# An FFN's inner layer in three-chunk rounds: a two-bank and a one-bank PSUM tile in turn, and an activation table named at the start

## The chip, the cores and the metric

The kernel runs on one core of a Trainium2 chip. The metric is the device time of one execution in microseconds, the median of several runs. The engines are named as the profile names them: PE (TensorE matmuls), PEld (TensorE weight loads), DVE (VectorE), ACT (ScalarE), POOL (GpSimd), SP (SyncE, which here issues most DMAs).

## The reference, cut to what matters

The input `x` has 4 images of 384 channels and 32 x 32 positions, so 1024 tokens per image. Two layers follow one another. Layer 0 is a selective scan in four directions (16 states per channel) with a GELU, then a mixture of four experts of which each token takes two. Layer 1 is self-attention with 8 heads, then a small FFN whose two weight matrices are Kronecker products:

```python
w_fc = jnp.kron(c_fc_1, c_fc_2)        # (1536, 32) x (1, 12)  -> (1536, 384)
w_proj = jnp.kron(c_proj_1, c_proj_2)  # (32, 1536) x (12, 1)  -> (384, 1536)
h = x @ w_fc.T
h = jax.nn.gelu(h, approximate=False)
out = h @ w_proj.T
```

The residual and a normalisation stand around each part. The change is in this last FFN. Because of the Kronecker form the kernel first folds 384 channels into 32 numbers per token (`z`), and the inner layer multiplies only those 32 numbers by the 1536 columns of `c_fc_1`.

## The kernel before, in words

Tokens are in the free dimension of the inner layer, in halves of 512 (`HF`), and the 1536 hidden units are 12 chunks (`FC`) of 128 partitions. One batch of the whole program is one image.

**The order of the work.** `scan_layer` (L192) walks over 32 units (image, direction, half). When the scan of an image ends, the function `between` (L1292) starts `tail_batch` of the image before it: experts, combine, attention and the last layers, while the next image's scan goes on. So the tails of images 0 and 1 run beneath the scans, that of image 2 straddles the end of the last scan, and that of image 3 comes last. The order on each engine is not written by hand: the whole program is handed to a planner that lays out a timeline with priorities when the kernel is built (`schedule_with_timeline_sim=True`, L1285). Parts inside `high_priority(offset=FORWARD)` go ahead of the scan's work whenever they are ready; routing (L603), the combine (L488) and the last layers (L495) are such parts. On an engine the instructions then run in that fixed order.

**Rooms and banks.** The tail draws its buffers from a `Room` (L88). On-chip buffers have tags with a number of buffers each: for images 0 to 2 `NARROW` (L78), with two `k12` buffers; for image 3 `WIDE` (L79), with three. PSUM has three tags: `s`, of two banks each (`two`, L107), `o` and `p`, of one bank each (`bank`, L104). Images 0 to 2 have one buffer of each tag (L84). The attention and last layers of image 3 have two of each (L85), which is all eight banks.

**The last layers** (`last_layers`, L1049). The attention's result is projected (L1083, `o_ps`), added to the tokens `xt` (L1087, a `k12` buffer that stays to the end), and normalised. `z` is made by L1091 to L1112. Then, for each half `i` of the tokens and for each group of six chunks, `hidden` (L1117) makes `hs`, a `k12` buffer: for three pairs of chunks, a pair of matmuls of 32 rows (L1123) into one two-bank tile of tag `s`, and one ACT copy of 1024 columns (L1127) into `hs`; then one ACT GELU over all 3072 columns (L1128), with a table load before it and one after it (`exp_again`, L141). Chunk `f` uses the rows `f % 4` of the 32-row strips. The six chunks of `hs` are then contracted into `f_acc` (tag `o`, L1136). After both groups, DVE copies `f_acc` to `fy` (L1141), and for each of the three channel blocks a one-bank tile `fo_ps` (tag `p`, L1143) takes 8 matmuls (L1146 and L1150), ACT copies it out (L1155) and a DMA stores it (L1156). There are thus four calls of `hidden` in an image and sixteen in the kernel.

Other users of tag `p` in the same room are the routing of the next image (`tt_ps`, L622; `cnt_ps`, L705), which runs beside the last layers of images 0 and 1, and the attention before them.

The other place that the change touches is the start of `Body.__init__`: ACT there issues the load of the packed constants `cols` (L123); `scan_layer` makes ACT issue the load of `wx` (L203), and the first activation is the exponential that makes `nega` (L206).

Of the kernel before, what the change touches and what calls it, by code (L numbers as in the profile page):

```python
# [87 lines left out]
class Room:  # L88


    def __init__(self, tc, ctx, name, bufs):
        self.tc, self.name, self.bufs = tc, name, bufs
        self.sb = ctx.enter_context(tc.tile_pool(name=name, bufs=1, reuse_waits="tile"))
# [17 lines left out]
def halves(i):  # L111
    return slice(i * HF, (i + 1) * HF)


class Body:
    def __init__(self, ctx, tc, a):
        self.tc, self.nc, self.a = tc, tc.nc, a
        nc = self.nc
        const = ctx.enter_context(tc.tile_pool(name="const", bufs=1))
        self.const = const  # L120

        self.cols = const.tile([P, NCOL], F32, tag="cols", name="cols")
        nc.scalar.dma_start(out=self.cols, in_=a["cols"])  # L123

        self.ident = const.tile([P, P], F32, tag="ident", name="ident")
        make_identity(nc, self.ident)
        self.ones = const.tile([P, P], F32, tag="ones", name="ones")
        nc.gpsimd.memset(self.ones, 1.0)
        self.eps5 = const.tile([P, 1], F32, tag="eps5", name="eps5")
        nc.gpsimd.memset(self.eps5, 1e-5)  # L130
        self.eps6 = const.tile([P, 1], F32, tag="eps6", name="eps6")
        nc.gpsimd.memset(self.eps6, 1e-6)

        self.minus1 = const.tile([P, 1], F32, tag="minus1", name="minus1")
        nc.gpsimd.memset(self.minus1, -1.0)

        self.c2sum = const.tile([P, 1], F32, tag="c2sum", name="c2sum")
        lo, hi = COL["c2"]
        nc.vector.tensor_reduce(self.c2sum, self.cols[:, lo:hi], AX.X, ALU.add)
# [909 lines left out]
    def last_layers(self, b, att, room):  # L1049
# [4 lines left out]
        nc, a = self.nc, self.a  # L1054
# [23 lines left out]
        for m in range(0, MB, 2):  # L1078
            ps = room.two("o_ps")
# [26 lines left out]
        ps = room.two("z_ps")  # L1106
# [8 lines left out]
        ng = 6  # L1115

        def hidden(i, at):  # L1117
            hs = room.tile([P, ng, HF], "k12", "hs")
            for f in range(at, at + ng, 2):
                ps = room.two("h_ps")  # L1120
                for o in range(2):
                    rows = slice((f + o) % nq * KR, ((f + o) % nq + 1) * KR)
                    nc.tensor.matmul(  # L1123
                        ps[:, o, :], fc1[rows, (f + o) // nq, :], z[rows, halves(i)],
                        start=True, stop=True,
                    )
                nc.scalar.copy(hs[:, f - at : f - at + 2, :], ps)  # L1127
            self.exp_again(nc.scalar.activation(hs, hs, AF.Gelu).ins)  # L1128
            return hs

        for i in range(NH):
            out = room.bank("o", "f_acc")
            for at in range(0, FC, ng):
                hs = hidden(i, at)
                for f in range(at, at + ng):
                    nc.tensor.matmul(  # L1136
                        out[f % nq * KR : (f % nq + 1) * KR, :], pj1[:, f, :], hs[:, f - at, :],
                        start=(f < nq), stop=(f >= FC - nq),
                    )
            y = room.tile([P, HF], "k4", "fy")  # L1140
            nc.vector.tensor_copy(y, out)  # L1141
            for c in range(DC):
                ps = room.bank("p", "fo_ps")  # L1143
                for j in range(HF // P):
                    cols = slice(j * P, (j + 1) * P)
                    nc.tensor.matmul(  # L1146
                        ps[:, cols], pj2[:, c * P : (c + 1) * P], y[:, cols],
                        start=True, stop=False,
                    )
                    nc.tensor.matmul(  # L1150
                        ps[:, cols], xt[:, i * (HF // P) + j, c * P : (c + 1) * P], self.ident,
                        start=False, stop=True,
                    )
                o = room.tile([P, HF], "k4", "out")
                nc.scalar.copy(o, ps)  # L1155
                nc.sync.dma_start(out=a["out"][b][c * P : (c + 1) * P, halves(i)], in_=o)  # L1156
# [229 lines left out]
```

## Time and profile before

| | |
|---|---|
| runs | 4482.89, 4482.44, 4480.09 us; median 4482.44 us |
| profiled execution | 4517.48 us, of which the span from the first to the last instruction is 4513.6 us |
| PE | 3440.6 us busy (76%), 13852 matmul instructions |
| DVE | 3010.8 us busy (67%) |
| POOL | 3037.0 us busy (67%) |
| ACT | 2534.3 us busy (56%) |
| L1123, the inner layer's matmuls | 192 instructions, two for each chunk of 512 columns |
| L1127, its copies | 48 of 1024 columns, 1010 ns mean |
| L1128, its GELUs | 16 of 3072 columns, 2763 ns mean, each with a table load of 1283 ns |
| last layers' `z` ready (L1112) | image 0 at 1891, 1 at 2992, 2 at 4135, 3 at 4450 us |

The busy time of an engine is what it spent in instructions, without its waits. The profiled execution is slower than the median of the runs by 35 us; its parts add up to its own time.

### The profile page before, as it was taken

To read this page: it belongs to the slowest core of one execution; us is meant where nothing else is said; L and a number is where in the kernel's file an instruction comes from. 1 tells how busy PE (TensorE), PEld (TensorE's weight loads), DVE (VectorE), ACT (ScalarE), POOL (GpSimd) and SP (SyncE) were. 2 spreads that over 40 slices of the span, in tenths; PEclk is the share of its full clock that TensorE was granted. 3 is DMA by queue.
4 is the path that set the end of the run, shared out by engine and by line. 5 is a ranking of instruction groups with operands and counts; after the bars stand their busy time and mean duration, and the time that the engine had idled before them with its cause. 6 is when DMAs were issued, how large, how long until landed. Compare 5 with 4: busy or idle time off the path is not lost. (4 is left out here: it accounts for less than half of the span.)

```text
span 4513.6 us, 46925 instructions
## 1 busy us (share of the span) xinstructions
PE 3440.6 (76%) x13852; PEld 1652.0 (37%) x13852; DVE 3010.8 (67%) x4344; ACT 2534.3 (56%) x4406; POOL 3037.0 (67%) x1467
## 2 busy tenths in 40 slices
PE   6545554479894787669998588757998689999796
PEld 2111121145552222225555222214555445556333
DVE  4999997878878977977877777896778520002102
ACT  4555554456665676466666577556666444334554
POOL 4999998788987877778988778878889510000100
PEclk7666665589996898669998699858999789999897
DMA  4444554477886533457779443445787543344200
GB/s 119 118 123 118 146 136 106 137 230 209 231 240 181 149 84 104 130 159 226 210 220 275 137 114 101 115 139 170 232 244 232 169 157 115 107 127 153 75 16 15
DMA packets 404361, 684.81 MB, mean 152 GB/s; under 512 B 50944, under 2 KB 206464, under 8 KB 404096
## 3 DMA queue, kind: packets, MB, share of 16 engines
q1 hardware_dynamic: 395360, 656.16, 50.3%
q0 software_dynamic: 8192, 25.17, 1.7%
q8 instruction: 111, 1.82, 0.2%
q14 instruction: 154, 1.26, 0.1%
q10 hardware_dynamic: 544, 0.40, 0.0%
HBM read 561.47 MB, written 120.06 MB: 151 GB/s over the span
## 5 line engine op out<-in xcount | busy, mean ns | idle before, releaser
L420 POOL TENSOR_TENSOR bx<-dtr,bcs 128x1024 f32<-128x1024 f32 x768 | 1797.8, 2366 | 227.7 <-PE acc L455 103.5
L429 ACT ACTIVATE da<-dtr,nega 128x512 f32<-128x512 f32 x1536 | 1045.5, 691 | 1039.4 <-DVE bx L441 569.0
L448 POOL TENSOR_TENSOR bx<-bx,bcs 128x1024 f32<-128x1024 f32 x384 | 903.6, 2358 | 211.8 <-DVE bx L434 88.0
L455 PE MATMUL acc<-bx,sel 128*32 128x512 f32 x3072 | 511.8, 713 | 312.4 <-POOL bx L448 248.8
L879 PE MATMUL h_ps<-xc,w 128*128 128x256 f32 (+1 forms) x3168 | 680.1, 370 | 61.7 <-DVE xc L861 31.5
L895 PE MATMUL y_ps<-w,hs 128*128 128x384 f32 x1824 | 649.9, 509 | 49.8 <-ACT hs L888 44.1
L879 PEld LDWEIGHTS h_ps<-xc,w 128*128 128x128 f32 x3168 | 557.2, 200 | 253.4 <-issue 120.4
L434 DVE TENSOR_TENSOR_SCAN bx<-da,carry,bx 128x512 f32<-128x512 f32 x384 | 474.0, 1269 | 118.6 <-POOL bx L420 65.5
L434 DVE TENSOR_TENSOR_SCAN bx<-da,bx 128x512 f32<-128x512 f32 x384 | 452.2, 1209 | 129.2 <-POOL bx L420 70.3
L434 DVE TENSOR_TENSOR_SCAN da<-da,carry,bx 128x512 f32<-128x512 f32 x384 | 476.5, 1273 | 67.9 <-ACT da L429 62.6
L441 DVE TENSOR_TENSOR bx<-da,bcs 128x512 f32<-128x512 f32 x768 | 509.8, 679 | 3.8
L434 DVE TENSOR_TENSOR_SCAN da<-da,bx 128x512 f32<-128x512 f32 x384 | 456.3, 1218 | 60.7 <-ACT da L429 44.2
L895 PEld LDWEIGHTS y_ps<-w,hs 128*128 128x128 f32 x1824 | 352.3, 198 | 341.7 <-issue 86.4
L992 ACT ACTIVATE ex<-s_ps 128x512 f32<-128x512 f32 x512 | 299.4, 591 | 274.9 <-PE s_ps L987 259.9
L987 PE MATMUL s_ps<-w 64*128 64x512 f32 x1024 | 308.4, 674 | 83.1 <-ACT ex L992 74.2
L1077 POOL TENSOR_TENSOR xt<-xt,wb 128x3072 f32<-128x3072 f32 x4 | 26.8, 6708 | 477.5 <-DMA w<-in_w 345.5
L1036 PE MATMUL o_acc<-ex,vt 128*64 128x512 f32 x1024 | 295.6, 658 | 0.8 <-ACT att L1044 0.8
L455 PEld LDWEIGHTS acc<-bx,sel 128*32 128x32 f32 x3072 | 77.7, 117 | 596.0 <-POOL bx L448 363.8
L884 ACT ACTIVATE hs<-h_ps,bb 128x256 f32<-128x256 f32 (+1 forms) x528 | 194.0, 447 | 128.8 <-PE h_ps L879 128.5
L899 DVE TENSOR_TENSOR y<-y_ps,bb 128x384 f32<-128x384 f32 x76 | 41.6, 548 | 237.6 <-PE y_ps L895 237.6
L913 POOL DMA_INDIRECT got<-made,g_pos x64 | 60.8, 950 | 192.4 <-PE f_acc L1136 159.1
L987 PEld LDWEIGHTS s_ps<-w 64*128 64x128 f32 x1024 | 81.1, 192 | 266.8 <-ACT ex L992 149.1
(216 smaller groups left out, 4021.9 us busy)
## 6 DMA issues: line engine op xcount, KB each, us to landing
w<-in_w SPq DMA_DIRECT2D x352, 576.0 KB
dtr<-dd SPq DMA_DIRECT2D x1536, 128.0 KB
bcs<-rows SPq DMA_DIRECT2D x512, 128.0 KB
dd<-one_e SPq DMA_DIRECT2D x96, 256.0 KB
dd<-mag SPq DMA_DIRECT2D x96, 256.0 KB
rows<-zero SPq DMA_DIRECT2D x76, 192.0 KB
xs<-rows SPq DMA_DIRECT2D x32, 384.0 KB
made<-y SPq DMA_DIRECT2D x32, 384.0 KB
```

Source lines behind the costliest of these rows:

```text
L420: pool = nc.gpsimd.tensor_mul(bx, dtr[q][1], bc[:, 0].unsqueeze(1).to_broadcast([P, 2, HF])).ins
L429: nc.scalar.activation(da, dtr[q][0][:, j, :], AF.Exp, scale=nega[:, col : col + 1])
L434: nc.vector.tensor_tensor_scan(run(h), run(da), run(bx[:, j, :]), 0.0 if first else hold, ALU.mult, ALU.add,)
L441: dve = nc.vector.tensor_mul(bx[:, j, :], h, cg).ins
L448: pool = nc.gpsimd.tensor_mul(bx, bx, cg.unsqueeze(1).to_broadcast([P, 2, HF])).ins
L455: nc.tensor.matmul(acc[lo : lo + DB, :], sel, out[q][:, j, :], start=(g == 0), stop=(g == NG - 1),)
L879: nc.tensor.matmul(ps[:, r, :], w1[(f + r) // wf][:, c, (f + r) % wf * P : ((f + r) % wf + 1) * P], xc[:, c, :], start=(c == 0), stop=(c = ...
L884: nc.scalar.activation(hs[:, f + r, :], ps[:, r, :], AF.Identity, bias=bb[:, f + r : f + r + 1])
L895: nc.tensor.matmul(out[:, :D], hs[:, f, t * P : (t + 1) * P], w2[f // wf][:, f % wf, :], start=(f == 0), stop=(f == FC - 1),)
L987: nc.tensor.matmul(ps[:, o, :], w[rows, j * P : (j + 1) * P], w[rows, halves(i)], start=True, stop=True,)
L992: ins = nc.scalar.activation(ex[:, o, :], ps[:, o, :], AF.Exp, scale=HD**-0.5, accum_out=sums[:, t, 2 * j + o, i : i + 1],).ins
L1036: ins = nc.tensor.matmul(out[cols, :], made[t][1][:, j, cols], ex[:, o, :], start=(j == 0), stop=(j == MB - 1),).ins
```

## The change

There are two edits. The first puts a load of the table set `natural_log_exp_and_others` at the head of ACT's program. The second takes the six chunks of `hidden` in the pattern two, one, two, one. The twos use a two-bank tile of tag `s`, the ones a one-bank tile of tag `p`; each tile is copied by one ACT instruction, so that a call of `hidden` has two copies of 1024 columns and two of 512 in place of three of 1024. The matmuls, the GELU and everything behind it are the same.

```diff
@@ -119,6 +119,8 @@
         const = ctx.enter_context(tc.tile_pool(name="const", bufs=1))
         self.const = const
 
+
+        nc.scalar.preload_act_table_set("natural_log_exp_and_others")
         self.cols = const.tile([P, NCOL], F32, tag="cols", name="cols")
         nc.scalar.dma_start(out=self.cols, in_=a["cols"])
 
@@ -1116,15 +1118,22 @@
 
         def hidden(i, at):
             hs = room.tile([P, ng, HF], "k12", "hs")
-            for f in range(at, at + ng, 2):
-                ps = room.two("h_ps")
-                for o in range(2):
+
+            f = at
+            while f < at + ng:
+                if (f - at) % 3 == 0:
+                    ps = room.two("h_ps")
+                else:
+                    ps = room.bank("p", "h_ps").unsqueeze(1)
+                n = ps.shape[1]
+                for o in range(n):
                     rows = slice((f + o) % nq * KR, ((f + o) % nq + 1) * KR)
                     nc.tensor.matmul(
                         ps[:, o, :], fc1[rows, (f + o) // nq, :], z[rows, halves(i)],
                         start=True, stop=True,
                     )
-                nc.scalar.copy(hs[:, f - at : f - at + 2, :], ps)
+                nc.scalar.copy(hs[:, f - at : f - at + n, :], ps)
+                f += n
             self.exp_again(nc.scalar.activation(hs, hs, AF.Gelu).ins)
             return hs
 
```

## The prediction

> **What bounds the kernel now.** First the page: the busy tenths in 40 slices of the span.
>
> ```profile
> PE   6545554479894787669998588757998689999796
> ...
> DVE  4999997878878977977877777896778520002102
> ...
> POOL 4999998788987877778988778878889510000100
> ```
>
> Two regimes. Up to about 3600 us POOL and DVE carry the scan, and the tails of images 0 and 1 run beneath it. After that POOL and DVE are nearly empty and PE is full, until the last layers of image 3. Does the FFN beneath the scan count at all? For this I read the chain that ended last around the FFN of image 1 (start, us, what).
>
> ```profile
> 3058.33 1.01 ACT hs L1127
> ...
> 3060.66 2.76 ACT hs L1128
> ...
> 3100.63 0.15 SPq L833
> ...
> 3101.10 4.65 DMA xs<-rows
> ```
>
> It does, at least in part: the chain runs through the FFN's copies and GELUs (and, in between, through the scan's DVE work) into the weight load and the gather with which the next image's experts begin. An FFN that ends sooner lets them begin sooner. Then the view of the inner layer's matmuls, what they wait for (us, times).
>
> ```profile
> L1123 PE MATMUL h_ps<-z,wc x192: 587/848/1218, 1892.6 to 4487.5; 32*128 32x512 f32 x192
> ...
>   ACT hs L1127: 100.9, 36
> ```
>
> The matmul stands behind the copy of the tile before it: PE and PEld together sat 100.9 us before L1123 for L1127. Last the timeline of the final stage.
>
> ```profile
> 4463.01 1.93 ACT L1127 COPY hs<-h_ps 128x1024 f32<-128x1024 f32 x2
> ...
> 4465.31 1.37 PE L1123 MATMUL h_ps<-z,wc 32*128 32x512 f32 x8
> 4466.72 1.01 ACT L1127 COPY hs<-h_ps 128x1024 f32<-128x1024 f32 x1 [1.78 <-PE h_ps L1123]
> 4467.75 1.28 ACT L1128 ACT_TABLE_LOAD   x1
> ...
> 4469.04 2.76 ACT L1128 ACTIVATE hs<-hs 128x3072 f32<-128x3072 f32 x1
> ```
>
> ACT makes two copies, then idles 1.78 us: the third pair found no free bank and was queued behind 3.63 us of L1136 on PE. Also: eight instructions (four chunks, four row strips) take 1.37 us, where the row of four (one pair) takes 1.13. Chunks of different strips run side by side.
>
> **The change part by part.** All against the profiled 4517.48 us.
>
> *The table load at the start.* The load is there already: 1.28 us at 1.69, before the first exponential (L206). It moves ahead of the two DMA issues of ACT's queue (0.75 and 1.20), which go 1.28 later. `cols` then lands near 5.1 instead of 3.8; c2sum, dsum and nega follow it. Cover: the first matmul waits for `u` until 8.05, and `wx` is not read before 34.6. If that cover went, it would cost 1.3. I take 0, bounds 0 and +1.3.
> The Trainium skill ("ScalarE: Activation LUTs", What ACT_TABLE_LOAD costs) counts 2.66 us for a switch, with a drain; here the GELU starts 1.29 us after its load starts (4467.75, 4469.04). By the page `cols` would land near 6.5, still before 8.05, so the sum is 0 by either.
>
> *The copies.* Two copies of 1024 in a row take 1.93, so 0.965 each; two of 512 in a row (L1155 at 4484.20) take 1.08, so 0.54. A call: 3 x 0.965 = 2.90 before, 2 x 0.965 + 2 x 0.54 = 3.01 after. The 0.11 is inside the sums below.
>
> *Last layers of image 3* (two `s`, two `p`). All six chunks find a bank, so PE can fill them during the GELU before. ACT is then the only chain: load 1.28, copies 3.01, load 1.28, GELU 2.76 = 8.33 from GELU to GELU. They now start at 4458.94, 4469.04, 4479.22, 4491.31: gaps of 10.10, 10.18, 12.09. That saves 1.8 and 1.9, and up to 3.8 in the last, where the outputs of the first half (L1155) are copied too and share tag `p`; I take 2.0 there. In the first call four chunks end together (4451.30 to 4453.39), the other two by 4455.46, copies to 4456.97, load: GELU at 4458.3, 0.7 sooner. Sum **-6.4**. Best case -8.2. Worst case, banks of tag `p` given strictly in program order: the third call's second single chunk waits for three `fo_ps`. After the GELU: L1136 3.65, `fy` to 4.39, two `fo_ps` of 1.92 each from 4.95, copy 0.6, the third 1.92 and 0.6, then chunk 1.13, copy 0.54, load 1.28, about 14.3 where it is 7.4 now: +6.9, so 0.6 in all (-0.7 - 1.8 + 6.9 - 3.8).
>
> *Image 2* (one `s`, one `p`, one `hs`: `xt` holds the other `k12` buffer). The last call runs its three copies from 4212.36 to 4220.42, 8.06 us, PE cold (pair 2.08). With a pair and a single ready: copy 1.0, pair 2.08 beside the single's copy, copies 1.0 and 0.58, about 4.7, plus two 0.58 copies of the combine between them: 5.9, so -2.2. The third call's last chunk waits for `fo_ps`, whose third ends on PE at 4199.8: copy 0.58, chunk 1.13, copy 0.58, load 1.28, GELU 4203.4 instead of 4201.74, +1.7. The first two calls stand among the experts' matmuls on a full PE: three bursts of 1.13 become two of about 1.25 (between 1.13 and 1.37), -0.9 each. Sum **-2.3**; bounds -6 (no such wait, and both late calls save 2.2) and +11 (below).
>
> *Images 0 and 1, beneath the scan.* Here a copy stands in ACT's queue among the scan's exponentials, which wait for DVE. From one copy to the next takes 9.5, 8.8, 7.9, 3.8, 3.5, 4.2, 7.4, 3.2 us (image 0, mean 6.0) and 5.7 in image 1. A pair and a single in flight make one such round per call instead of two. Upper end: 5.8 less a short copy, 5.2 for each of three calls, -15.6. Lower end: pair and copy without scan work, 1.7 (warm) to 2.6 (cold), -6.3. Against it, the third call's last chunk behind three `fo_ps`: L1155 of the first at 1967.71, two more at about 3.0, chunk, copy and load, GELU at 1977.3 instead of 1971.10, +6.2. So -9.4 to 0, I take -5 for each image. How much reaches the end is not shown; the chain above alternates between tail and scan, so I take half: **-5** for both; ends -19 and (below) +15.
>
> Extra waits: the chunk waiting for tag `p` stands on PE ahead of L455, whose result frees the scan's buffers (POOL L420 waited for L455 103.5 us over the run), and ahead of routing's L708. No row shows that wait alone.
>
> A page speaks against all this. The Trainium skill ("TensorE: Matmul & The Clock Gate", HAM oscillation — how this bites in real kernels) reports that double-buffering PSUM in a thin matmul kernel brought nothing further (126.6 to 125.5 us). By it the sum would be 0 and the time 4482; the row of 1.78 us idle before the third copy speaks for a gain.
>
> **Sum**: 0 - 6.4 - 2.3 - 5 = -13.7 on 4517.48, the profiled execution's own time; the runs' median is 0.992 of that, so 4482.44 - 13.6 = **4469**.
>
> **Rivals.**
>
> *Only the end gains (chance 0.27).* Beneath the scan POOL and DVE decide, and an earlier FFN changes nothing. For: the chain there goes through L434 and L429 too. Against: it also goes through L1128. Then -6.4 alone, 4476, within 0.2%, which is about what a measurement of this kernel can tell from no change.
>
> *Slower: the one bank of tag `p` (0.20).* In images 0 to 2 the third call's last single chunk queues behind three outputs that keep today's pace.
>
> ```profile
> 1967.71 0.58 ACT L1155 COPY out<-fo_ps 128x512 f32<-128x512 f32 x1 [2.14 <-PE fo_ps L1150]
> ...
> 1971.10 2.76 ACT L1128 ACTIVATE hs<-hs 128x3072 f32<-128x3072 f32 x1
> ...
> 1975.66 0.59 ACT L1155 COPY out<-fo_ps 128x512 f32<-128x512 f32 x1
> ...
> 1982.79 0.58 ACT L1155 COPY out<-fo_ps 128x512 f32<-128x512 f32 x1
> ```
>
> Today two outputs are copied after that GELU. If it must wait for the third: 1982.79 + 0.58 + 1.13 + 0.58 + 1.28 = 1986.4 less 1971.1, +15; image 1 (3070.29, GELU 3060.66) +13; image 2 (4209.35, 4201.74) +11. Against it the other three calls save at least 6.3 in each. Half of (15 + 13 - 12.6), plus 11 - 6.3, plus 0.6 at the end: +13, 4495. It decides once the wait exceeds those 6.3. Against: without the GELU in between ACT is free for the outputs.
>
> *The tiles don't run side by side (0.08).* The planner puts other work between pair and single, so a call is four bursts of up to 1.13 on PE instead of three. In images 2 and 3 PE is on the path: 8 x 1.13 = +9, less the 6.4: 4485.
>
> Besides, any new order moves the whole scan: from one scan's end to the next it took 942.8 (to 2673.5) and 918.1 us (to 3591.6) with like work beneath, 24.7 apart. This sits on every case with either sign.
>
> **How the numbers follow.** Forecast 0.45. Below, its upper ends give -8.2 - 6 - 19 = -33, 4449; above, the slower rival gives 4495. Range 4449 to 4495, the forecast's own about 4449 to 4480. Faster by over 0.2% (under 4473.5): 0.40 of the forecast's 0.45 and 0.10 of the others through the new order, 0.50. Slower (over 4491.4): 0.15 of the bank rival, 0.07 of the rest, 0.22. Within: 0.28.
>
> **What would show it.** Right: in the last layers of image 3 gaps near 8.3 between GELUs, no idle before copies; in images 0 to 2 fewer and shorter waits of L1123 for L1127; experts after them starting sooner. Wrong: L1123 waiting for L1155, a GELU of the third call after all three outputs, or POOL waiting longer for L455.

## The result, and the profile after

The changed kernel took 4519.66 us (median; 4515.14 to 4526.06) beside 4481.26 us for the kernel before: a ratio of 1.0086, 95% interval 1.0073 to 1.0098. It is slower by 38 us; 4469 was forecast, and 4495 was the upper end of the range.

In the changed kernel the lines are numbered higher, by 2 up to the last layers: L1131 is the inner layer's matmul, L1135 its copies, L1137 the GELU, L1145 `f_acc`, L1164 the output copies, L457 the scan's reduction on PE, L710 and L711 the counts of routing, L713 their copy.

First the page, the busy tenths in 40 slices.

```profile
PE   6545554479894787669898588757899879999797
...
DVE  4999998878878976977877868896777730002102
...
POOL 4999998788988877778988769777888720000100
```

POOL is busy into the 33rd slice (7 and 2 in slices 32 and 33, where it was 5 and 1): the last scan ended at 3624 us, where it was 3595. Yet the two profiled spans are 4513.5 and 4513.6 us. They can't be set against each other: the kernel before alone has a median of 4480 or 4481 us on some chips and 4511 to 4518 on others, and its profiled execution (4517.48) lies with the second, while its own runs (4480 to 4483) lie with the first. Below, kernels are compared by the ratio to the kernel before beside which they ran, and traces, where one is at hand, with one of before on a chip of like time. Even the ratio carries over only roughly: the same changed kernel gave 1.0086 here and 1.0061 on a chip where before takes 4511 us (e5 below).

Then the view of the inner layer's matmuls, what PE and PEld waited for in the changed kernel.

```profile
L1131 PE MATMUL h_ps<-z,wc x192: 587/1056/1218, 1889.8 to 4485.1; 32*128 32x512 f32 x192
...
  ACT hs L1135: 152.2, 50
  DVE z L1114: 30.6, 6
  DVE g_cnt L713: 12.6, 2
  ACT out L1164: 6.9, 6
```

The wait for copies, 100.9 us in 36 waits before, is 152.2 in 50 (on chips of like time, e13 and e5 below: 110.9 in 36 and 147.9 in 46). Two new ones stand beside it: for the copy of routing's counts (`g_cnt`) and for the output copies. Both are users of tag `p`.

Last the timeline of ACT in the last layers of image 3.

```profile
4458.23 2.76 ACT L1137 ACTIVATE hs<-hs 128x3072 f32<-128x3072 f32 x1
...
4462.31 2.91 ACT L1135 COPY hs<-h_ps 128x1024 f32<-128x1024 f32 x4
4465.23 1.28 ACT L1137 ACT_TABLE_LOAD   x1
4466.53 2.76 ACT L1137 ACTIVATE hs<-hs 128x3072 f32<-128x3072 f32 x1
...
4476.83 0.59 ACT L1164 COPY out<-fo_ps 128x512 f32<-128x512 f32 x1 [0.84 <-PE fo_ps L1159]
4478.62 0.59 ACT L1164 COPY out<-fo_ps 128x512 f32<-128x512 f32 x1 [1.20 <-PE fo_ps L1159]
4481.65 0.59 ACT L1164 COPY out<-fo_ps 128x512 f32<-128x512 f32 x1 [2.44 <-DMA out<-out]
4482.13 0.59 ACT L1135 COPY hs<-h_ps 128x512 f32<-128x512 f32 x1
4483.44 0.59 ACT L1135 COPY hs<-h_ps 128x512 f32<-128x512 f32 x1 [0.72 <-PE h_ps L1131]
...
4485.34 2.76 ACT L1137 ACTIVATE hs<-hs 128x3072 f32<-128x3072 f32 x1
...
4491.80 2.76 ACT L1137 ACTIVATE hs<-hs 128x3072 f32<-128x3072 f32 x1
```

From the first GELU to the second the four copies follow one another without a gap, 2.91 us, and the distance is 8.30 us where it was 10.10. The third call's single chunks come after all three outputs: 18.81 us where it was 10.18. The last distance is 6.46 in place of 12.09. From `z` to the last GELU it is 41.5 us, as before (41.3).

### The profile page after: what moved, and what is told of

Its sections match the earlier page's. It is cut to its first block, busy times and chain, and to the rows that moved or that the text cites. A ratio compares the mean times of both kernels' runs of the same rounds, so it can differ in the third digit from the quotient of the medians.

```text
span 4513.5 us, 46922 instructions
## 1 busy us (share of the span) xinstructions
PE 3452.7 (76%) x13852; PEld 1649.9 (37%) x13852; DVE 3044.1 (67%) x4344; ACT 2537.7 (56%) x4422; POOL 3034.8 (67%) x1467
## 5 line engine op out<-in xcount | busy, mean ns | idle before, releaser
L422 POOL TENSOR_TENSOR bx<-dtr,bcs 128x1024 f32<-128x1024 f32 x768 | 1797.8, 2369 | 225.3 <-PE acc L457 119.8
L450 POOL TENSOR_TENSOR bx<-bx,bcs 128x1024 f32<-128x1024 f32 x384 | 906.9, 2366 | 226.9 <-DVE carry L447 93.0
L457 PE MATMUL acc<-bx,sel 128*32 128x512 f32 x3072 | 510.7, 719 | 306.7 <-POOL bx L450 263.2
L881 PE MATMUL h_ps<-xc,w 128*128 128x256 f32 (+1 forms) x3168 | 674.0, 367 | 62.6 <-DVE xc L863 29.4
L897 PE MATMUL y_ps<-w,hs 128*128 128x384 f32 x1824 | 643.3, 505 | 42.4 <-ACT hs L890 37.3
L457 PEld LDWEIGHTS acc<-bx,sel 128*32 128x32 f32 x3072 | 77.1, 117 | 600.7 <-POOL bx L450 387.0
L347 PE MATMUL dt_ps<-xd,wdt 12*128 12x512 f32 x192 | 130.8, 767 | 64.5 <-ACT mag L386 37.6
```

The lines of the kernel that those rows point to most:

```text
L422: pool = nc.gpsimd.tensor_mul(bx, dtr[q][1], bc[:, 0].unsqueeze(1).to_broadcast([P, 2, HF])).ins
L450: pool = nc.gpsimd.tensor_mul(bx, bx, cg.unsqueeze(1).to_broadcast([P, 2, HF])).ins
L457: nc.tensor.matmul(acc[lo : lo + DB, :], sel, out[q][:, j, :], start=(g == 0), stop=(g == NG - 1),)
L881: nc.tensor.matmul(ps[:, r, :], w1[(f + r) // wf][:, c, (f + r) % wf * P : ((f + r) % wf + 1) * P], xc[:, c, :], start=(c == 0), stop=(c = ...
L897: nc.tensor.matmul(out[:, :D], hs[:, f, t * P : (t + 1) * P], w2[f // wf][:, f % wf, :], start=(f == 0), stop=(f == FC - 1),)
```

## The experiments

Theory A: the one bank of tag `p` makes the FFNs beneath the scans longer, and that is the loss. Theory B: the planner lays out everything behind the first changed instruction anew, and the time goes with that order, whatever the edit was. The table collects what the runs gave; each is taken up below. "FFN" is the time from the start of the last step of `z` to the start of the last output copy, in images 0 to 3; "scans" are images 2 and 3, each from the end of the scan before it to its own end (the last L228); "rest" runs from there to the end of the span.

| run | ratio to before (95% interval) | FFN, us | scans 2, 3, us | rest, us |
|---|---|---|---|---|
| e1 before | 1.0010 (1.0000-1.0019) | 119.9 111.3 104.8 56.6 | 944.9 914.7 | 919.8 |
| e13 before | 0.9995 (0.9986-1.0004) | 119.0 110.6 102.2 57.1 | 945.1 916.6 | 914.0 |
| e5 the change | 1.0061 (1.0045-1.0078) | 149.5 136.3 109.7 53.7 | 967.3 938.3 | 892.9 |
| e3 image 0 | 0.9984 (0.9975-0.9994) | 150.7 118.0 98.5 57.6 | 969.2 909.9 | 891.9 |
| e4 image 1 | 1.0030 (1.0020-1.0040) | 119.8 126.7 107.1 54.7 | 947.7 915.9 | 928.0 |
| e8 image 2 | 1.0007 (0.9997-1.0017) | 119.4 111.3 103.5 57.5 | 947.4 915.4 | 915.6 |
| e2 image 3 | 0.9996 (0.9986-1.0005) | 117.7 111.6 102.1 53.3 | 945.5 914.2 | 911.0 |
| e12 images 0, 1 | 1.0070 (1.0056-1.0083) | 144.5 132.9 104.2 54.4 | 960.4 925.8 | 883.6 |
| e17 images 0, 1, ones first | 1.0105 (1.0090-1.0119) | 151.0 130.0 101.7 57.8 | 958.8 908.7 | 926.6 |
| e6 first call in pairs | 1.0080 (1.0063-1.0096) | 130.7 131.9 125.3 54.6 | 979.3 934.8 | 902.4 |
| e10 third call in pairs | 0.9988 (0.9976-0.9999) | 131.5 125.0 101.2 53.8 | 965.7 905.3 | 865.2 |
| e15 second and fourth call only | 1.0034 (1.0023-1.0046) | 117.3 122.6 102.6 53.9 | 972.5 929.4 | 895.0 |
| e7 control, image 0 | 0.9976 (0.9965-0.9986) | 120.1 118.9 103.1 57.3 | 958.8 902.8 | 894.1 |
| e11 control, image 1 | 0.9947 (0.9933-0.9961) | 116.9 110.3 98.1 57.7 | 935.1 895.7 | 887.3 |
| e14 control, images 0, 1 | 0.9982 (0.9973-0.9991) | 122.5 121.7 103.8 56.9 | 972.5 906.9 | 893.6 |
| e18 control, images 0, 1, last pairs | 1.0023 (1.0013-1.0033) | 120.2 110.7 106.2 57.3 | 959.7 903.8 | 893.0 |
| e9 control, all images | 1.0022 (1.0013-1.0032) | 117.6 119.3 101.4 57.9 | 972.7 900.6 | 892.9 |
| e16 control in 1, calls 2 and 4 in 3 | 0.9927 (0.9914-0.9940) | 120.4 114.8 101.9 54.1 | 948.6 915.1 | 892.1 |

The kernel before took 4511 us beside e1 to e8 and 4518 beside e13 to e16, but 4480 and 4481 beside e9 to e12, e17 and e18. In the runs on these faster chips, e9 to e12, e17 and e18, the columns in us are about 30 us lower in all for that.

**The kernel before again, and the change in one image at a time.** e1 is the kernel before. e2, e3, e4 and e8 have the changed pattern in one image (3, 0, 1, 2) and pairs in the others:

```diff
-                if (f - at) % 3 == 0:
+                if (f - at) % 3 == 0 or b != 3:
```

> The kernel before, unchanged, for a second profile and a second median: the profiled execution shown of it took 4517.5 us where its runs took 4481, so its stages can't be set beside those of the changed kernel without knowing where the 35 us lie. Expected by every theory: a median within 4 us of 4481 (ratio 1.000). If the first profile was an odd one, this profiled execution takes 4480 to 4490 and ends the last scan (last L228) about 3560, or has the 35 us less after it; if profiling itself slows this kernel, it takes 4515 again.

> The two-one pattern in the last layers of image 3 alone (two banks of tag p), pairs in images 0 to 2; the early table load stays. Everything ahead of these last layers keeps the order of the kernel before. The prediction's step: 6.4 us less, 4475. The one-bank theory: the profile of the changed kernel shows the third call's single chunks behind the three fo_ps (gaps between GELUs 8.3, 18.8, 6.5 where they were 10.1, 10.2, 12.1), so the stage gives nothing, 4481 plus or minus 3. If the 38 us lie at the end, 4510 or more.

> The pattern in the last layers of image 0 alone. One-bank theory: the first call's single chunks wait for routing's counts (cnt_ps) in the one bank of tag p and its GELU comes about 23 us later, the FFN ends about 22 us later, the next experts and the rest follow: 4490 to 4505. Order theory (any new order moves the scan, whatever the waits): between 4457 and 4507 with no tie to the FFN's end. Prediction's step: 4476 to 4482.

> The pattern in the last layers of image 1 alone. One-bank theory: first GELU about 25 us later than z allows in the kernel before, FFN's end about 27 us later, and as image 1's experts and attention feed straight into the stage after the scan, 4495 to 4510. Order theory: between 4457 and 4507. Prediction's step: 4476 to 4482.

> The change in image 2 alone (pairs in images 0, 1 and 3). The forecast had -2.3 us here with bounds -6 and +11: a ratio of 0.9995, between 0.9987 and 1.0024. Theory A: the third call's single chunk waits for three outputs, and that shows at the end, as PE is full: about +11, 1.0024. Theory B: everything ahead of this FFN is in the old order, so nothing moves before 4130 us; behind it the order of image 3's tail is new, worth at most some 5 us either way (0.999 to 1.001).

e1 was expected at 4481 us by every theory and took 4515.65, beside 4511 for the same kernel; so the times expected of e2, e3 and e4 in us are to be read as differences from 4481. e1 and e13 show how well the same program repeats: 0.1%. Image 3 alone gained 3.3 us in its FFN and nothing that the time can tell. Image 0's FFN was 31 us longer, and the time 0.16% *shorter*: the scan of image 2 took 24 us more, and the rest, with the same 3415 matmuls, 28 us less, where theory A expected 9 to 24 us more in all. Image 1's FFN was 15 us longer and the time 0.3% longer, but its scans were as before; the loss lies in the rest. So the FFN's delay doesn't simply appear at the end. Image 2 alone is nothing that the time can tell; theory A expected 1.0024.

**The whole change again.**

> The whole change once more, beside the kernel before on one chip. Theory A (the one bank of tag p): in the changed kernel's trace the FFNs of images 0 and 1 end 22.5 and 31.3 us later than in before's; if such delays reach the end, the ratio is that of the first result, about 1.008. Theory B (a new order: each FFN is later, but what reaches the end depends on how everything behind it is laid out anew): the single images gave 0.9984 (image 0), 1.003 (image 1) and 0.9996 (image 3) against before; if they add up, with image 2 at nothing, 1.001; anything from 0.997 to 1.006 would fit B, and 1.008 would leave 0.006 to image 2 and to what the parts do together.

On a chip where before takes 4511 us the change takes 4541.65, a ratio of 1.0061; the single images add up to 1.0017. The rest, 0.0044, comes only when they are together. The spans cut at the ends of the scans, first before (e13), then the change (e5); the columns are the stretch, its length, busy us of PE, PEld, DVE, ACT and POOL with their instructions, the granted clock, the DMA share and GB/s.

```profile
1735.10:2680.20 945.10, 732.36 (x3051) 375.06 (x3049) 749.77 (x1078) 585.32 (x961) 776.56 (x376) 0.84 0.62 181
2680.20:3596.80 916.60, 737.66 (x3117) 370.87 (x3113) 720.62 (x1016) 563.15 (x966) 747.98 (x361) 0.87 0.59 172
3596.80:4510.80 914.00, 809.48 (x3415) 413.50 (x3415) 122.04 (x293) 399.69 (x836) 49.16 (x39) 0.93 0.31 99
```

```profile
1734.80:2702.10 967.30, 758.14 (x3117) 381.06 (x3116) 770.09 (x1080) 591.98 (x983) 777.00 (x376) 0.83 0.60 176
2702.10:3640.40 938.30, 743.40 (x3048) 372.50 (x3046) 737.80 (x1022) 562.20 (x957) 745.64 (x361) 0.84 0.58 169
3640.40:4533.30 892.90, 807.13 (x3415) 411.82 (x3415) 119.57 (x285) 398.48 (x840) 49.31 (x39) 0.93 0.31 101
```

Both scans are 22 us longer, and the stage behind them 21 shorter with the same 3415 matmuls. In it PE was busy 809.5 and 807.1 us, so the 21 us are nearly all idle time that went (104.5 to 85.8). POOL was busy as long as before in both scans (776.6 and 777.0, 748.0 and 745.6), but DVE 20 and 17 us longer, with about as many instructions; where that comes from is taken up behind the controls.

**Where the FFN became longer.** The PE timeline of image 0's first call, before (e13), then changed (e5).

```profile
1897.70 2.08 PE L1123 MATMUL h_ps<-z,wc 32*128 32x512 f32 x4
...
1906.28 2.07 PE L1123 MATMUL h_ps<-z,wc 32*128 32x512 f32 x4 [4.36 <-ACT hs L1127]
...
1917.87 0.63 PE L708 MATMUL cnt_ps<-g_rank,before_i 128*128 128x32 f32 x2 [5.06 <-DVE g_rank L697]
```

```profile
1898.28 2.08 PE L1131 MATMUL h_ps<-z,wc 32*128 32x512 f32 x4
...
1906.87 2.07 PE L1131 MATMUL h_ps<-z,wc 32*128 32x512 f32 x4 [4.36 <-ACT hs L1135]
...
1918.51 0.63 PE L710 MATMUL cnt_ps<-g_rank,before_i 128*128 128x32 f32 x2 [5.11 <-DVE g_rank L699]
...
1921.37 2.07 PE L1131 MATMUL h_ps<-z,wc 32*128 32x512 f32 x2
...
1929.48 2.07 PE L1131 MATMUL h_ps<-z,wc 32*128 32x512 f32 x2 [4.18 <-ACT hs L1135]
```

The pairs come at the same times as before (0.6 us later, as `z` is). The two single chunks come after the counts, though no PE instruction in this stretch ahead of L710 uses tag `p`, and then one after the other, as there is one bank. A single chunk (x2) holds PE for 2.07 us, as long as a pair (x4): the two chunks of a pair run beside each other. And each round ends in a copy that stands among the scan's exponentials (ACT of e5):

```profile
1905.81 1.00 ACT L1135 COPY hs<-h_ps 128x1024 f32<-128x1024 f32 x1
...
1928.87 0.56 ACT L1135 COPY hs<-h_ps 128x512 f32<-128x512 f32 x1
...
1940.07 0.69 ACT L431 ACTIVATE da<-dtr,nega 128x512 f32<-128x512 f32 x1 [6.46 <-DVE bx L436]
1940.70 0.58 ACT L1135 COPY hs<-h_ps 128x512 f32<-128x512 f32 x1
...
1943.25 2.76 ACT L1137 ACTIVATE hs<-hs 128x3072 f32<-128x3072 f32 x1
```

The last copy is behind an exponential that waits 6.46 us for DVE. The GELU starts at 1943.25, before (e13) at 1916.36. Measured from `z`, image 0's four GELUs in e5 against e13: first +26.3, then gaps of 20.80 (34.72 before), 34.65 (18.23), 21.03 (21.48). Image 1: first +20.2, gaps 26.88 (28.63), 28.53 (18.93), 17.38 (20.47). The pattern loses in the first call, behind the counts, and in the third, behind the three outputs. ACT of e5 in image 0's third call:

```profile
1987.55 0.59 ACT L1164 COPY out<-fo_ps 128x512 f32<-128x512 f32 x1 [2.91 <-PE fo_ps L1159]
1992.01 0.58 ACT L1164 COPY out<-fo_ps 128x512 f32<-128x512 f32 x1
1993.80 0.59 ACT L1135 COPY hs<-h_ps 128x512 f32<-128x512 f32 x1 [0.61 <-PE h_ps L1131]
...
1998.70 2.76 ACT L1137 ACTIVATE hs<-hs 128x3072 f32<-128x3072 f32 x1
```

The single's copy and the GELU come after the last of the three outputs, where before the GELU stood ahead of two of them. In the second and fourth call the gaps are shorter, in part because the call before came later (e15 below).

Not all of image 1's delay is the bank's. Its first GELU comes 43.0 us behind `z` in e5 and 22.8 in e13, but 38.4 in e4, where image 1 is the first to be changed, and 38.0 in the control e7 below, where no new tile uses tag `p`. Image 0's, ahead of which nothing has moved, is the clean case: 51.1 to 51.3 in every run with singles in its first call, 25.0 to 25.1 in every other.

**Undoing one call.** e6 and e10 put the first and the third call of every image back into pairs; e15 leaves the pattern in the second and fourth alone.

```diff
-                if (f - at) % 3 == 0:
+                if (f - at) % 3 == 0 or (i == 0 and at == 0):   # e6
+                if (f - at) % 3 == 0 or (i == 1 and at == 0):   # e10
+                if (f - at) % 3 == 0 or at == 0:                # e15
```

> The change with the first of the four calls of each image in pairs, as before; the other three calls take the pattern. In the changed kernel the first GELU of images 0 and 1 is 23.4 and 25.1 us later than before, and the first call's single chunk starts on PE just after the copy of routing's counts, which hold the one bank of tag p. Theory A: without that, the first GELU comes as early as before and the FFNs of images 0 and 1 end at most some 7 us later (the third call's wait for three outputs), so the time lies between before and 0.2% above it, and at least 0.3% under the changed kernel. Theory B: the first GELU comes as early, too, but the end moves by up to 15 us either way without regard to it.

> The change with the third of the four calls of each image in pairs, so that no chunk waits for the three outputs of the first half. The first call, whose single chunks wait for each other and for routing's counts, is as in the changed kernel. Theory A, with the forecast's rival (the third call's wait is what costs): clearly under the changed kernel's 1.0061, at 1.003 or less. If the first call's wait is what lengthens the FFN: FFNs of images 0 and 1 still 20 us or more longer than before's 119.9 and 111.3, and a ratio near 1.005. Theory B: the ratio is no guide; the FFNs may be shorter and the time longer, as with the first call in pairs (1.008).

> The pattern in the second and fourth call of every image alone; the first and third in pairs. In the changed kernel the time from GELU to GELU fell at these two calls (image 0: 34.58 to 20.79, though part of it is that the first came later, and 22.43 to 21.04; image 2: 21.90 to 13.23 and 20.85 to 15.62; image 3: 10.11 to 8.29 and 12.09 to 6.46), and rose at the third by 13.0, 8.7, 16.6 and 8.6. Theory A: all four FFNs last as long as before's or up to 10 us less (image 3: 52 to 54 in place of 56.6), and the time is below before: 0.998 to 0.9995. Theory B: the FFNs are as A says, and the ratio is anything from 0.994 to 1.006 all the same.

In image 0 the calls do what the timeline says: the FFN goes from 149.5 to 130.7 without the first call's singles, to 131.5 without the third's, to 117.3 without both. Image 1's goes from 136.3 to 131.9, 125.0 and 122.6, in e15 still 12 us above e13's, though neither call has singles there; with no singles at all it is 121.7 in the control e14 below. In e15, where the calls before them are in pairs, the second and fourth gap are 31.21 and 20.47 in image 0 (34.72 and 21.48 in e13), 29.09 and 24.83 in image 1 (28.63 and 20.47): the pattern gains little there.

From one run to the next the time doesn't follow the FFN. With the first call in pairs it is 1.008, where theory A expected at most 1.002; with the third 0.9988, as A expected; with both 1.0034, where A expected a gain, and image 0's FFN is no longer than before. e10 isn't slower than before with FFNs of images 0 and 1 that are 12 and 14 us longer. Theory A in its simple form, that the length of the FFNs sets the loss, falls here; what is left of it comes up behind the controls.

**The controls: a new order and nothing else.** These are the kernel before with pairs everywhere and no new use of tag `p`; only the copy of a pair is made by two instructions, in image 0 (e7), 1 (e11), both (e14), all (e9), or for the last pair of a call in images 0 and 1 (e18).

```diff
-                nc.scalar.copy(hs[:, f - at : f - at + 2, :], ps)
+                if b == 0:
+                    for o in range(2):
+                        nc.scalar.copy(hs[:, f - at + o, :], ps[:, o, :])
+                else:
+                    nc.scalar.copy(hs[:, f - at : f - at + 2, :], ps)
```

> The kernel before, with each pair of image 0's last layers copied by two instructions of 512 columns in place of one of 1024. No tile changes and nothing uses tag p that did not; it adds twelve copies of about 0.54 us in place of twelve halves of 0.965, 0.06 us each, 0.7 us in all. It is a change of order and nothing else: the planner lays out everything behind it anew. Theory A: no more than 0.7 us, a ratio of 1.0002. Theory B: the end moves by 5 us or more, either way (under 0.999 or over 1.001), and the times at which the scans end move by more than 5 us.

> As the run with image 0's copies split, but in image 1: nothing but twelve more copies, 0.7 us of ACT, and a new order behind image 1's last layers. Theory A: 1.0002 at most. Theory B: the end moves by over 5 us either way (under 0.999 or over 1.001), and the change in image 1 alone (1.003) is then mostly such a move.

> The kernel before with the pairs of all four images copied by two instructions of 512 columns each: 48 more copies of ACT, 0.06 us for each pair, 2.9 us in all, no use of tag p, and each FFN should last as long as before (119.9, 111.3, 104.8 and 56.6 us from z to the last output copy in images 0 to 3), give or take 5. Theory A (FFNs that are made later by tag p cost time, and the four add up to the changed kernel's 1.0061): 1.0006 at most. Theory B (any new order moves the scans and the stage behind them by tens of us, whatever it is): the scans of images 2 and 3 and the stage behind them differ from before's (944.9, 914.7 and 919.8 us) by over 10 us each in at least two of the three, and the ratio is anything from 0.995 to 1.006.

> The kernel before with the copies of images 0 and 1 split in two, no use of tag p: the control to the change in images 0 and 1 (1.007). Theory A (the longer FFNs beneath the scans make the loss): FFNs as long as before's, and a ratio of 1.001 at most, 0.005 or more under the change's. Theory B alone (any new order is worth up to 0.6% either way, the pattern has no sign of its own): anything from 0.994 to 1.007.

Twelve copies more, worth 0.7 us, moved the time by -0.24% in image 0 and by -0.53% in image 1; the other controls gave +0.22, -0.18 and +0.23%. Theory B holds in so far: an order alone is worth some 24 us down to 10 us up. But none of the five controls is as slow as the change. An order alone also makes an FFN longer: image 1's is 118.9 in e7, 119.3 in e9 and 121.7 in e14, 8 to 11 us above e13's 110.6. In e7 the scan of image 2 took 13.7 us more than in e13 and that of image 3 13.8 less, and the rest 19.9 less. The scans don't carry the same tail work in every order: beneath these two PE ran 3051 and 3117 matmuls in e13, 3117 and 3048 in e5, 3175 and 2991 in e7. So part of such a shift is work that went from one stretch into another; e10's short rest of 865.2 us has 3347 matmuls in place of 3415.

**What an order does to a scan.** The tail's DVE instructions meet POOL's differently. The eight instructions that normalise `xt` ahead of image 1's attention, before (e13), DVE:

```profile
2575.08 5.21 DVE L531 TENSOR_SCALAR xt<-xt,mv,rstd 128x384 f32<-128x384 f32 x8
2580.21 2.45 DVE L434 TENSOR_TENSOR_SCAN da<-da,carry,bx 128x512 f32<-128x512 f32 x2
```

The same in the changed kernel (e5), DVE, and then POOL in the same stretch:

```profile
2560.54 15.07 DVE L533 TENSOR_SCALAR xt<-xt,mv,rstd 128x384 f32<-128x384 f32 x8
2575.53 2.45 DVE L436 TENSOR_TENSOR_SCAN bx<-da,carry,bx 128x512 f32<-128x512 f32 x2
```

```profile
2560.17 14.44 POOL L422 TENSOR_TENSOR bx<-dtr,bcs 128x1024 f32<-128x1024 f32 x6 [2.60 <-PE acc L457]
```

They took 15.07 us in place of 5.21, for as long as POOL ran six instructions without a gap, and the scan's next DVE instruction starts when they are done. A sum of 128 x 16 numbers in the attention shows it more strongly: 0.17 us in e13, 11.46 in e5.

```profile
2818.43 0.17 DVE L1000 TENSOR_TENSOR inv<-sums 128x16 f32<-128x16 f32 x1 [0.29 <-ACT ex L992]
```

```profile
2821.77 11.46 DVE L1002 TENSOR_TENSOR inv<-sums 128x16 f32<-128x16 f32 x1 [3.26 <-ACT ex L994]
2833.16 2.45 DVE L436 TENSOR_TENSOR_SCAN da<-da,carry,bx 128x512 f32<-128x512 f32 x2
```

Of all DVE instructions, what each took beyond the shortest of its line and shape, counted where that is over 1 us, comes in the scans of images 2 and 3 to 24.4 and 29.4 us in e13, and 42.4 and 45.4 in e5. In e5 95% and in e13 98% of the time of these instructions lies beside a running POOL instruction; of all DVE time in these scans 81 and 83% does. That is 18 and 16 us more, where the scans became 22 and 22 longer. By this sum, most of what the change added to the scans would be tail work on DVE that now falls where POOL is busy without a gap. But the sum doesn't set the length of a scan: e3 has almost as much of it (40.6 and 44.4, in all 31 us more than e13), and its two scans are 17 us longer together; the controls e7 (26.5 and 40.3) and e14 (33.6 and 40.3) had shorter scans of image 3 than e13 all the same (902.8 and 906.9); e6 has 27.4 in the scan of image 2 and took 34 us longer for it. No run takes this cost away by itself, so its share is argued, not shown.

The Trainium skill, "SBUF — State Buffer", Who interferes with whom, has a rule for this: DVE instructions with two SBUF inputs, or in a two-port mode as `tensor_scalar` can be, need ports that POOL shares, and whichever of the two comes second is blocked for the whole instruction of the other. The trace agrees on who is slowed (a `tensor_scalar`, an addition of two SBUF tiles); the wait, though, outlasted one instruction: 11.46 us is almost five of POOL's instructions of 2.3 us. In e13 the 0.17 us fell into a pause of POOL, from 2817.38 to 2821.86.

**The change against its control.** e12 has the change in images 0 and 1, e17 the same with the singles first:

```diff
-                if (f - at) % 3 == 0:
+                if b > 1 or (f - at) % 3 == 1:
```

> The change in images 0 and 1, pairs in 2 and 3. Image 0 alone gave 0.9984, image 1 alone 1.003, the whole change 1.0061. If the parts add up: 1.0014. If the two FFNs beneath the scans make the loss together, for instance because the scan of image 3 is longer (938.3 us in the changed kernel, 914.7 before, 909.9 and 915.9 with one image changed): 1.005 to 1.0065, and images 2 and 3 are worth nothing. Theory B allows either, and says that the parts don't add up in general.

> A second draw of the change in images 0 and 1: the pattern one, two, one, two in place of two, one, two, one, pairs in images 2 and 3. The tiles and their tags are the same kinds, four rounds in place of three where the one-bank tile has to wait, and the order behind it is another one. If the longer FFNs beneath the scans cost something whatever the order (theory A's core): FFNs of images 0 and 1 longer than 119.0 and 110.6 us by 10 or more, and a ratio over 1.003 again (the first draw gave 1.007). If it is the order alone (theory B): anything from 0.994 to 1.006, as likely below 1 as above.

> A second draw of the control: the kernel before, in images 0 and 1 the last pair of each call copied by two instructions of 512, eight more copies of 0.06 us net, no use of tag p. Theory A's core: FFNs as long as before's, at or under 1.002, and under the other run of this call by 0.003 or more. Theory B alone: anything from 0.994 to 1.006, and no sign in the difference to the other run.

e12 gives 1.0070, beside 1.0086 for the whole change on a chip of like time: images 0 and 1 together make most or all of the loss. In each comparison of the same images the change stands above the control: image 0 0.9984 and 0.9976, image 1 1.0030 and 0.9947, all images 1.0061 and 1.0022, images 0 and 1 1.0070 and 0.9982, and the second draw 1.0105 and 1.0023. That is five of five, by 0.0008 to 0.0088, but it is no proof. The comparisons share images. Only the last two runs shared a chip; for image 0 the intervals overlap, and between chips a ratio moved by 0.0025 (1.0086 and 1.0061). The strongest single point is e17, announced as a test: at 1.0105 it lies outside the 0.994 to 1.006 that theory B gave, and 0.0082 above its control. So the runs point to a cost of the pattern beneath the scans besides the order, between nothing and 0.9%.

The table as a whole points the same way. Over its sixteen changed kernels the time rises with the four FFNs' lengths added up: the correlation is 0.74, with about 0.7 us for each us of FFN and a scatter of 15 us, which is as much as an order moved the controls. That is a correlation only: the runs share edits and come from several chips, and an order that delays other work can delay an FFN with it. Where the cost arises the runs don't show. In e5 the scans are longer. e17 and e18 end their last scans within 3.5 us of each other, and 33.6 of the 37.1 us between their spans lie in the rest (926.6 us with 3415 matmuls, 893.0 with 3375).

The scan's progress shows the direct part in image 0. The same instruction of POOL's L420 starts 19.8 us later in e5 than in e13 just behind the FFN (the one at 2075 us in e13), 9.5 later at 2278, and then, before image 1's FFN begins, 48.1 later at 2979. Most of the lateness grows between the FFNs, and there an order alone makes it, too: in the control e14 the same three instructions start 6.8, 4.9 and 42.7 us later than in e13.

**The kernel before once more, and a version that beats both.** e13 is before; e16 has image 1's copies split, and in image 3 the pattern in the second and fourth call.

```diff
-                if (f - at) % 3 == 0:
+                if (f - at) % 3 == 0 or b != 3 or at == 0:
...
-                nc.scalar.copy(hs[:, f - at : f - at + n, :], ps)
+                for o in range(n if b == 1 else 1):
+                    w = n if b != 1 else 1
+                    nc.scalar.copy(hs[:, f - at + o : f - at + o + w, :], ps[:, o : o + w, :])
```

> The kernel before, for a profile beside the runs of this call: on two chips it took 4511 us, on others 4480. If this call's time is near 4480, its scans and the stage behind them (on a chip of 4511: 796.3, 939.4, 944.9, 914.7 and 919.8 us) show where the 30 us lie. If they lie in the granted clock, the stage behind the scans is shorter; if in memory, the scans are.

> A version meant to beat both kernels: image 1's copies split in two (0.9947 when alone), and in image 3 the pattern in the second and fourth call alone (worth some 3 us of its 56.6 by the gaps of 8.29 and, at the end, 6.46 to 8.3 in place of 10.11 and 12.09). The parts lie behind one another, and the last changes nothing ahead of 4380 us: 0.9947 less 0.0007, so 0.993 to 0.995. If it is above 0.997, the 0.9947 is not a property of the order alone.

e16 took 4487.57 us beside 4518.03, 0.9927 (0.9914 to 0.994): faster than both kernels. Image 3's FFN, 54.1, has the 3 us expected of it, but not where they were expected: the second call's gap is 7.31 us (10.43 in e13), the fourth's 13.05 (12.08), as its singles are copied after the three outputs there (4464.88, then 4466.86). The other 0.5% is an order that happens to be better, and holds on a second chip; there is no reason in it to carry away. e13's run was on a chip of 4518 and so said nothing of the faster ones.

## Why the prediction was wrong

- **Images 0 and 1** were the failed step: "A pair and a single in flight make one such round per call instead of two", -5 us in all. It didn't hold in the first call: the single had to wait for routing's counts, which the forecast saw only from the other side (the chunk standing ahead of L708), and the two singles then took a round each, four rounds in place of three. In the third call both singles waited for the three outputs. The FFNs became 30 and 26 us longer, not shorter; image 0's is shown to be the pattern's doing (e6, e10 and e15 take it back), of image 1's 26 us only 15 are there when it is changed alone (e4), and an order alone gave 8 to 11 (e7, e9, e14). In the second and fourth call it held only in part: 3.5 and 1.0 us gained in image 0 of e15, 0.5 and 4.4 lost in image 1.
- **The time** is another matter. That these FFNs make the 38 us is not shown: image 0's FFN, 31 us longer, went with a time 7 us shorter (e3). So "half" of the FFN's gain reaching the end can't be relied on in a single kernel; over all of them some 0.7 us went with each us of FFN, with a scatter of 15 us. The cause of the loss as a whole stays open between the order and the pattern.
- **The rival of the one bank** named the right tag and, for the third call, the right wait and size: +15 and +13 for the GELU, where the gap before it grew by 16.4 and 9.6. It failed on the other side of its sum: "the other three calls save at least 6.3 in each". The first lost 26 us in image 0 and, alone (e4), 16 in image 1. With the measured FFNs its rule of one half would give about 4515 in place of 4495 (half of 30.5 and 25.7, plus 7.5 in image 2, less 3.4 in image 3); close to 4520. e6 fits that rule as well (37 us by it, 36 measured), e3 and e10 don't (16 and 9 us by it, 7 and 5 us *shorter* measured), so the closeness is in part luck.
- **"Any new order moves the whole scan"** was written down with 24.7 us, and that was the right size: the controls cover 34 us (-24 to +10). But it was used only to spread the chances between faster and slower; in the sum it stood at nothing, and the range was not widened by it. With 24.7 above the rival's 4495 it would just have held the 4519.66.
- **The extra waits** ahead of L455 were named without a price. POOL's wait for it went from 103.5 us over the run to 119.8 (L457 in the changed kernel). The forecast took such a rise for a sign that the one bank costs time; but it is 128.1 and 132.4 in the controls e7 and e14, without the new use of tag `p` and with shorter times, so the sign doesn't tell the two apart.
- **Image 3**: -6.4 was forecast, the FFN lost 3.3 us of 56.6 (e2). Gaps of 8.33 were forecast for the second call, measured 8.29. The third was the worst case named, 6.9 more: it was 8.6 more. The last gained more than thought, 5.6 in place of 3.8, since during the wait for the outputs its pairs were already made and copied. In the first call the GELU came 1.0 us sooner, where 0.7 was forecast (8.91 and 7.91 us behind `z`). At the end it can't be told from nothing (0.9996). With the second and fourth call alone the FFN keeps the 3 us (e16).
- **Image 2**: -2.3 with bounds of -6 and +11; alone -1.3 against e1 (103.5 and 104.8), in the whole change 109.7, inside the bounds, with no effect on the time (1.0007).
- **The table load at the start**: no run has it alone. It is in e2, e3, e4 and e8, whose first scan ends at 792.7 to 796.1 us, in e1 and e13 at 796.3 and 795.6; nothing of 1.3 us or more can be made out, and with it e2 and e8 took 0.9996 and 1.0007.
- **The Trainium skill**, "TensorE: Matmul & The Clock Gate", HAM oscillation, was set against the change: double-buffering PSUM brought nothing there. Where both tiles had a bank of their own (image 3, second call) the gap did fall, 10.10 to 8.30 us in the profiled runs, so the row was the better guide for the stage; for the time of the whole kernel the page's "nothing further" came closer than the forecast, though not for its reason.

Not settled: how the 38 us divide between the order and the pattern, how much of the longer scans is DVE behind POOL, why the rest became shorter, and whether a us of FFN beneath a scan itself costs the 0.7 us that go with it. The singles from tag `o` in place of `p` would have tested the bank by itself; no run has that.

## What to carry to other kernels

A small tile from a tag that other stages use is no free bank: list who holds the tag at that moment, in the order in which the planner hands it out, and count rounds of matmul and copy, each with its place in the busy engine's queue. Where a planner lays out the whole program, make a control that changes the order and nothing else before believing in any effect of under 0.6%, and take more than one draw of both. Small DVE instructions that land beside a POOL without gaps may be one way in which an order costs: look for the same line with durations of 0.2 and 10 us. Compare only what ran beside each other on one chip, traces included.

## What the runs showed of the hardware that was not expected

The same program takes 4480 us on some chips and 4511 to 4518 on others. e11 and e16 have the same sequence of instructions on DVE and POOL through the whole program, and on PE up to image 3's last layers (4401 us in e11). Their scans of images 1, 2 and 3, first e11 beside a before of 4480 us, then e16 beside one of 4518 (columns as in the stretches above):

```profile
796.30:1735.90 939.60, 718.87 (x2967) 351.90 (x2959) 754.48 (x1048) 570.29 (x1007) 765.81 (x375) 0.84 0.62 178
1735.90:2671.00 935.10, 729.93 (x3051) 374.16 (x3049) 750.03 (x1078) 585.43 (x962) 775.56 (x376) 0.85 0.62 182
2671.00:3566.70 895.70, 733.69 (x3115) 367.87 (x3113) 721.18 (x1020) 566.45 (x981) 748.70 (x362) 0.88 0.61 177
```

```profile
796.60:1736.20 939.60, 716.59 (x2967) 350.40 (x2959) 754.78 (x1048) 570.48 (x1007) 766.17 (x375) 0.84 0.62 178
1736.20:2684.80 948.60, 733.45 (x3051) 375.79 (x3049) 750.65 (x1078) 585.69 (x962) 776.34 (x376) 0.84 0.62 180
2684.80:3599.90 915.10, 739.96 (x3115) 371.93 (x3113) 720.63 (x1020) 567.02 (x981) 748.92 (x362) 0.86 0.60 173
```

The scan of image 1 takes the same 939.6 us on both; those of images 2 and 3 differ by 13.5 and 19.4, with busy times of DVE, ACT and POOL within 0.8 us. On these three engines the 33 us are waits; PE was busy 3.5 and 6.3 us longer on the slower chip. There the granted clock is a hundredth or two lower (0.84 and 0.86 against 0.85 and 0.88), and DMA moved a little less per second (180 and 173 GB/s against 182 and 177); which of these is the cause, and which the effect of a longer scan, the runs don't show.
